# Seven half products for eight in the weight products of a four-layer graph network

## The chip, the cores and the metric
The kernel runs on one core of a Trainium2 chip. A core has a matrix engine (TensorE, PE in the profile), a vector engine (VectorE, DVE), a scalar engine (ScalarE, ACT), GpSimd (POOL) and SyncE (SP), which here only issues transfers. The metric is the device time of one launch in microseconds. Everything is float32, and N = 2708 nodes with D = 512 features are worked on.

## The reference
Four layers follow one another, and each is wrapped in a residual and a layer norm:

```python
deg = jnp.maximum((adj != 0).astype(jnp.float32).sum(-1), 1.0)
x = layernorm(x + layer0(x))   # relu((dinv*(adj + I)*dinv @ x + x) @ W0 + b0)
x = layernorm(x + layer1(x))   # (dis*adj*dis @ x) @ W1.T + b1
x = layernorm(x + layer2(x))   # twice: proj = x @ W; Wh, Ws = split(proj)
                               #   a = softmax(Wh @ Ws.T) * adj; x = leaky_relu(a @ Wh + x)
x = layernorm(x + layer3(x))   # adj @ (x @ W3) + b3, all heads side by side
```

The three dense layers (0, 1 and 3) each have one product with the sparse 2708 x 2708 adjacency and one with a 512 x 512 weight. Layer 2 has two attention layers, each with its own projection.

## The kernel before
**Chunks.** The 2708 nodes are cut into six chunks of columns (`CH`): four of 512 (called wide here), then 384 and 276 (narrow). They also form 22 blocks of 128 rows (the last one has 20). A wide chunk has four blocks. The adjacency product of a chunk goes over six groups of row blocks (`GROUPS`): `multiply(ly, k, g)` adds one group into four PSUM banks, one for each 128 of the features. It takes the rows of x split in two parts, hi and lo, and the adjacency tiles `m`, which ACT casts from bytes or from float32. PSUM is used as two halves of four banks, and the chunks take turns on them (`bank(half, name)`).

**A dense layer.** `step` does one group of one chunk. After the last group `evict` writes `ht` (the transposed result) from PSUM to SBUF. The products with the weights are not made at once: `step` calls `ends(run, phase)` for the chunk before, one phase after each group of the chunk now running. Phase 0, after the first group, is `project`: for each block of 128 rows four matmuls of 128 x 128 by 128 x 512 into a bank `mm`. It also combines the first two blocks. Phase 1, after the second group, combines the rest and calls `finish`, which normalizes and writes rows `o`. In layer 1 phase 2, after the third group, turns `o` on TensorE (`tr_x2t`) for the attention. `combine` takes a block's `mm`, scale and bias into `r`, adds the residual `xres`, and gets statistics for the norm; the root `rs_t` of the norm is an ACT instruction, and the rest is on DVE.

**Attention.** For each chunk `project_steps` makes `wst`, the product of `mixed` (a product of the two halves of W, made early) with the chunk's `xt`, in four banks of four matmuls, and then `z`, the product of `xt` with W's first half, one bank for each row block. ACT copies `wst` and `z` to SBUF. `sum_weights` then adds and subtracts quarters of `wst` on DVE, because the attention's score products (`spx`, `spy`) are made in a seven-product form already. Of the first attention layer, chunks 0 and 1 are projected at the end of layer 1 by `project`, which calls `beat` after each step, and chunks 2 to 5 at the start of the attention itself. The second attention layer's projections are spread through the first one's scores.

**Index jobs.** From layer 1 on, lists of neighbours are made in the background. `work("DVE")` and `work("PE")` let the next piece of such a job go, on DVE (`at_row`, `marks`, and smaller pieces) or on TensorE (`list`, `rank`, `rest`). `beat` calls `work` in two of three calls. A `list` product waits for the `marks` before it.

**Order.** Every engine carries out its instructions in the order in which the program issues them: `OrderedEngine` adds a dependency from each instruction to the one before it on its engine, with no semaphore. Since this helper records them all, each instruction stands at line 71 in the profile, and is told apart by its tiles. An engine that waits keeps everything behind it waiting. The order that matters is written out by hand in `step`, `ends` and `project_steps`.

```python
for i, lo, n in sorted(blocks_of(k), key=lambda b: b[2] > QW):
    ...
    ps = self.bank(k, f"mm{ly.number}_{i}")
    for c in range(DC):
        nc.tensor.matmul(ps[:n], ly.ht[k][c][:, lo : lo + n], ly.w[c], ...)
    parts.append((i, n, ps))
```

Of the kernel before, what the change touches and what calls it, by code (L numbers as in the profile page):

```python
# [8 lines left out]
FP = mybir.dt.float32  # L9
# [475 lines left out]
    return {4: (1, P), 5: (1, P)}.get(k, (2, 2 * P))  # L485


STREAMED = 4
FIRST_LANDS = 16
SOFT = NB + 2 * 2  # L490
ALONE = 18
SEVEN = [0, 1]


def lists_of(i):
# [9 lines left out]
    return 4 * columns / 2400  # L505


class Layer:


    def __init__(self, number, source, weights, bias):
        self.number, self.source, self.weights, self.bias = number, source, weights, bias
        self.hi, self.lo = [None] * NB, [None] * NB
        self.rows = [None] * NB
        self.acc, self.ht, self.done, self.part = {}, {}, {}, {}
        self.mv = {}
        self.begun = {}
        self.loaded = set()


# [10 lines left out]
class Fast:  # L531
# [18 lines left out]
    def run(self):  # L550
        kernel, nc = self.k, self.nc
        with ExitStack() as ctx:
            pool = lambda name, bufs, **kw: ctx.enter_context(
                self.tc.tile_pool(name=name, bufs=bufs, reuse_waits="tile", **kw)
            )
            self.pages, self.wides = pool("pages", PAGES), pool("wides", WIDES)
            self.small = pool("small_f", 4)
            self.banks = [pool(f"banks{h}", 4, space=PSUM) for h in range(2)]
            given = [kernel.x_in[bass.ts(i, P), :] for i in range(NB)]
            l0 = Layer(0, given, kernel.w0, kernel.b0)  # L560
            l1 = Layer(1, kernel.saved[0], kernel.w1, kernel.b1)
            l3 = Layer(3, kernel.saved[2], kernel.w3, kernel.b3)
            self.attention = attention = Attention(self)
            self.jobs, self.due, self.other, self.beats = [], None, 1, 0
            run = Run(l0, l1)
            for t in range(len(run.seq)):
                self.step(run, t)
            attention.project(attention.layers[0], 0)
            for g in range(3):
                self.ends(run, g)  # L570
                if g == 1:
                    attention.project(attention.layers[0], 1)


            run = Run(l3)
            run.seq = [(l3, k, g) for k in range(TWO) for g in range(4)]
            run.seq += [(l3, k, g) for g in (4, 5) for k in range(2)]
            run.seq += [(l3, k, g) for k in range(2, TWO) for g in (4, 5)]
            run.seq += [(l3, k, g) for k in range(TWO, len(CH)) for g in range(len(GROUPS))]
            attention.run(self.early(run))  # L580
            for j in range(*GROUPS[5]):
                l3.rows[j] = attention.made[j]
            for t in range(4 * TWO, len(run.seq)):
                self.step(run, t)

            ly, k = run.before
            parts = self.project(ly, k)
            for some in (parts[:-1], parts[-1:]):
                made = []
                for i, n, ps in some:  # L590
                    made.append((i, n, self.combine(ly, k, len(made), i, n, ps)))
                self.finish(ly, k, made)
# [141 lines left out]
    def load_weights(self, ly):  # L734
        nc = self.nc
        ly.w = []
        for c in range(DC):
            w = self.page(f"w{ly.number}_{c}")
            nc.gpsimd.dma_start(w, ly.weights[bass.ts(c, P), :])
            ly.w.append(w)  # L740
        ly.bt = self.page(f"bias{ly.number}")
        nc.gpsimd.dma_start(ly.bt, ly.bias.partition_broadcast(P))

    def load_rows(self, ly, j):
        if ly.rows[j] is None:
# [210 lines left out]
    def degree_ends(self, ly, k):  # L956
# [22 lines left out]
        for c in range(DC):  # L979
            nc.gpsimd.tensor_mul(xt[c][:, :cw], xt[c][:, :cw], dg[:, :cw])  # L980
        yield True
        for _ in self.rsqrt(self.k.dis[:, i0 : i0 + n], cnt, DEG_EPS):
            pass
        nc.vector.tensor_scalar_max(cnt, cnt, 1.0)
        nc.vector.reciprocal(self.k.rdeg[:, i0 : i0 + n], cnt)

    def evict(self, ly, k):
        nc, cw = self.nc, CH[k][1]
# [12 lines left out]
            ht.append(t)  # L1001
        del ly.acc[k]

    def project(self, ly, k):

        nc = self.nc
        parts = []

        for i, lo, n in sorted(blocks_of(k), key=lambda b: b[2] > QW):
            if n <= QW:  # L1010
                ps = self.few(
                    k,
                    f"mm{ly.number}_{i}",
                    n,
                    D,
                    lambda c: ly.ht[k][c][:, lo : lo + n],
                    lambda c: ly.w[c],
                )
                parts.append((i, n, ps))
                continue  # L1020
            ps = self.bank(k, f"mm{ly.number}_{i}")
            for c in range(DC):
                nc.tensor.matmul(
                    ps[:n],
                    ly.ht[k][c][:, lo : lo + n],
                    ly.w[c],
                    start=(c == 0),
                    stop=(c == DC - 1),
                )
            parts.append((i, n, ps))  # L1030
        return parts
# [20 lines left out]
        return x  # L1052

    def sum(self, ly, i, n, ps):
        nc, x = self.nc, ly.done.pop(("xres", i))
        if n <= QW and ly.number == 3:
            for c in range(DC):
                nc.vector.tensor_add(x[:n], x[:n], ps[c * QW : c * QW + n, :])
# [79 lines left out]
    def step(self, run, t):  # L1138
# [3 lines left out]
        self.before_products(run, t)  # L1142
        if ly.number == 0 and (k, g) == (1, 0):
            self.attention.blank()
        if ly.number == 1 and k == len(CH) - 1 and g in (2, 3, 4):
            self.attention.begin(g - 2)
        if ly.number == 0 and g == len(GROUPS) - 1:
            self.multiply(ly, k, g, ds=range(2))
            ends = self.degree_ends(ly, k)
            next(ends)  # L1150
            self.multiply(ly, k, g, ds=range(2, DC))
        else:
            self.multiply(ly, k, g)
        if g == len(GROUPS) - 1 and k in ly.begun:
            self.evict(ly, k)
        wide = CH[k][1] == BANK
        if run.before and run.phase in ((1, 3, 4, 5) if wide else (1, 5)):
            self.work("PE")
# [11 lines left out]
        if g == len(GROUPS) - 1:  # L1170
# [10 lines left out]
            while run.before and run.phase < 2:  # L1181
                self.ends(run, run.phase)
                run.phase += 1
            if k in ly.acc:
                self.evict(ly, k)
            if ly.number == 0:
                for _ in ends:
                    pass
                self.checked()
            run.before, run.phase = (ly, k), 0  # L1190
            if ly.number == 0 and k == len(CH) - 1:
                note()
                self.load_weights(run.layers[1])
            if ly.number == 1:
                self.jobs.append((k, self.index(k)))
                self.work("DVE")
# [207 lines left out]
class AttentionLayer:  # L1404
    def __init__(self, number, pairs):
        self.number, self.pairs = number, pairs
        self.w, self.mixed, self.xt, self.wst = [], [], {}, {}
        self.sums, self.streamed, self.plain = {}, {}, set()


class Attention:
# [119 lines left out]
    def project(self, ly, k):  # L1531
        for _ in self.project_steps(ly, k):
            self.f.beat()

    def project_steps(self, ly, k):

        nc, a, cw = self.nc, ly.number, CH[k][1]
        xt = ly.xt[k]
        ly.wst[k] = []
        for m in range(DC):  # L1540
# [11 lines left out]
            ly.wst[k].append(t)  # L1552
            self.advance(DC * cost(cw))
            yield True
        self.sum_weights(ly, k)
        for i, lo, n in blocks_of(k):
            z = self.page(f"z_sb{a}_{i}")
            if n <= QW:
                ps = self.f.few(
                    0, f"z{a}_{i}", n, D, lambda c: xt[c][:, lo : lo + n], lambda c: ly.w[c]  # L1560
                )
                self.f.total(z[:n], ps, n, D)
            else:
                ps = self.bank(0, f"z{a}_{i}")
            for c in range(DC if n > QW else 0):
                nc.tensor.matmul(
                    ps[:n],
                    xt[c][:, lo : lo + n],
                    ly.w[c],
                    start=(c == 0),  # L1570
                    stop=(c == DC - 1),
                )
            if n > QW and a == 0:
                nc.scalar.copy(z[:n], ps[:n])
            elif n > QW:
                nc.vector.tensor_copy(z[:n], ps[:n])
            for b in range(2):
                rows = ly.pairs[b][i * P : i * P + n, :]
                nc.sync.dma_start(
                    bass.AP(rows.tensor, rows.offset, [rows.ap[0], (PAIR, 3), (1, D)]),  # L1580
                    z[:n].unsqueeze(1).to_broadcast([n, 3, D]),
                )
            self.advance((DC if n > QW else 1) * cost(D))
            yield True


    def quarters(self, ly, k):
# [80 lines left out]
    def replace_moving(self, ch):  # L1668
# [2 lines left out]
        for c in range(2):  # L1671
            self.nc.vector.tensor_sub(ch.part["t3"][c], ch.part["b22"][c], ch.part["t3"][c])

    PRODUCTS = {
        1: ("a11", "b11"),
        2: ("a12", "b21"),
        3: ("s4", "b22"),
        4: ("a22", "t4"),
        5: ("s1", "t1"),
        6: ("s2", "t2"),  # L1680
        7: ("s3", "t3"),
    }

    def product(self, ch, t, n, out, start=False):

        b, (w, x) = t["b"], self.PRODUCTS[n]
        for c in range(2):
            self.nc.tensor.matmul(
                out,
# [609 lines left out]
```

## Time and profile before

| what | value |
|---|---|
| median of 3 runs | 2304.07 us (2301.69 to 2308.27) |
| profiled execution | 2294.53 us, span 2292.7 us |
| TensorE busy | 2247.8 us (98%) |
| DVE busy | 1477.7 us (64%) |
| ACT busy | 691.1 us (30%) |
| POOL busy | 714.4 us (31%) |
| mean granted TensorE clock | 0.995 |
| matmuls `mm` of 512 columns | 504 records, 219.5 us |
| matmuls `z` of 512 columns | 336 records, 149.3 us |
| matmuls `wst` of 512 columns | 256 records, 114.2 us |

The span is that of one profiled execution, some 0.4% shorter than the median of the timed runs. A float32 matmul leaves two records in the trace[...]. A record's duration holds its own start and drain and overlaps the next record; the distance between two starts is what it costs in a stream. A group's line gives busy time and mean duration, then the idle time of its engine just before its instructions, and what ended that idle time. `mm` is from all three dense layers, `wst` and `z` are from both attention layers.

### The profile page before, as it was taken

Reading aid. Unit: us, or ns where it says so; the run is one execution under the profiler, and the core shown is the slowest. Engines: PE = TensorE matmul, PEld = TensorE weight load, DVE = VectorE, ACT = ScalarE, POOL = GpSimd, SP = SyncE. Lnnn points to the kernel's source line nnn. Section 1 sums busy time; section 2 is a strip of 40 time slices with the busy share of each in tenths; the row PEclk is TensorE's granted clock in tenths of the full one; section 3 lists DMA queues with packets and bytes.
Section 4 is the critical chain, followed back from the end, with each engine's and each line's share of the span. In section 5 each row is a group of like instructions: output and inputs, shape, how many; then the busy total and the mean of one; then the engine's idle time right before and its main releaser. Section 6 shows DMA issues by size and latency. Waiting matters only on the chain.

```text
span 2292.7 us, 27402 instructions
## 1 busy us (share of the span) xinstructions
PE 2247.8 (98%) x9004; PEld 1383.1 (60%) x9004; DVE 1477.7 (64%) x3012; ACT 691.1 (30%) x1474; POOL 714.4 (31%) x827
## 2 busy tenths in 40 slices
PE   9999999999999999999999999999999998899997
PEld 6677777777644787443555444687443455466685
DVE  6667787786664759866577522459859778625523
ACT  7444452222111234322222200134222323331221
POOL 2333441111000000556466550000566556643000
PEclk9999999999999999999999999999999999999999
DMA  9976762222557604889699999704879799974311
GB/s 332 294 203 166 201 185 81 77 81 86 205 192 274 243 28 153 285 283 312 224 324 364 323 410 349 260 24 150 273 264 348 256 317 345 319 231 133 113 48 43
DMA packets 274761, 504.27 MB, mean 220 GB/s; under 512 B 41774, under 2 KB 133606, under 8 KB 274608
## 3 DMA queue, kind: packets, MB, share of 16 engines
q1 hardware_dynamic: 205952, 287.46, 36.1%
q0 software_dynamic: 68656, 214.96, 29.0%
q8 instruction: 73, 1.20, 0.2%
q14 instruction: 80, 0.66, 0.1%
HBM read 316.47 MB, written 185.83 MB: 219 GB/s over the span
## 4 chain that ended last, share of the span: by engine, by line
PE 77%; DVE 8%; DMA 7%; issue 3%; ACT 2%; SPq 1%; POOL 1%; another core or an unknown queue 0%; DVEq 0%; ACTq 0%; POOLq 0%
PE acc L71 28%; PE sp L71 18%; PE mm L71 8%; PE spx L71 6%; PE z L71 5%; PE wst L71 5%; PE spy L71 4%; DVE s L71 2%; DMA pairs<-s 1%; DMA at<-in_adj_t 1%; DMA g<-pairs,givers 1%; DVE sum L71 1%; SPq L71 1%; DMA xt<-t 1%; DMA x<-in_x 1%
## 5 line engine op out<-in xcount | busy, mean ns | idle before, releaser
L71 POOL DMA_INDIRECT g<-pairs,givers x510 | 532.8, 1045 | 867.8 <-issue 373.5
L71 PE MATMUL acc<-m,xh 128*128 128x512 f32 (+4 forms) x1584 | 567.3, 379 | 3.6 <-ACT m L71 2.5
L71 PE MATMUL acc<-m,xl 128*128 128x512 f32 (+4 forms) x1584 | 550.7, 365 | 6.5 <-issue 5.8
L71 PE MATMUL sp<-xs,wst_sb 128*128 128x512 f32 (+5 forms) x1472 | 523.7, 525 | 0.0
L71 PEld LDWEIGHTS sp<-xs,wst_sb 128*128 128x128 f32 (+1 forms) x1472 | 260.7, 185 | 249.7 <-issue 186.2
L71 PEld LDWEIGHTS acc<-m,xh 128*128 128x128 f32 (+1 forms) x1584 | 288.6, 188 | 67.0 <-issue 20.8
L71 PEld LDWEIGHTS acc<-m,xl 128*128 128x128 f32 (+1 forms) x1584 | 289.1, 189 | 51.3 <-issue 11.6
L71 PE MATMUL acc<-g 128*32 128x512 f32 (+1 forms) x1020 | 270.4, 606 | 6.8 <-DMA g<-pairs,givers 4.7
L71 PE MATMUL mm<-w,ht 128*128 128x512 f32 (+1 forms) x528 | 223.1, 593 | 0.0
L71 ACT COPY s<-sp 128x512 f32<-128x512 f32 (+2 forms) x172 | 87.4, 509 | 439.4 <-PE sp L71 249.2
L71 ACT CAST m<-at 128x512 fp32r<-128x512 uint8 (+5 forms) x396 | 198.9, 567 | 43.9 <-DMA at<-mask 27.1
L71 DVE TENSOR_TENSOR sum<-sum,s 128x512 f32<-128x512 f32 (+4 forms) x252 | 157.3, 624 | 58.6 <-ACT s L71 37.2
L71 DVE TENSOR_TENSOR s<-s,a 128x512 f32<-128x512 f32 (+3 forms) x264 | 166.2, 629 | 9.2
L71 PEld LDWEIGHTS acc<-g 128*32 128x32 f32 (+1 forms) x1020 | 76.0, 134 | 156.8 <-issue 117.2
L71 ACT ACTIVATE s<-s 128x512 f32<-128x512 f32 (+3 forms) x264 | 147.2, 580 | 68.5 <-DVE s L71 42.2
L71 DVE TENSOR_TENSOR s<-s,shift 128x512 f32<-128x512 f32 (+3 forms) x264 | 162.4, 619 | 6.6 <-issue 5.1
L71 PEld LDWEIGHTS mm<-w,ht 128*128 128x128 f32 (+1 forms) x528 | 95.7, 186 | 116.5 <-issue 112.2
L71 DVE TENSOR_TENSOR top<-top,s 128x512 f32<-128x512 f32 (+3 forms) x240 | 149.3, 622 | 20.0 <-ACT s L71 11.9
L71 PE MATMUL wst<-xt,mixed 128*128 128x512 f32 (+2 forms) x384 | 150.7, 545 | 1.6 <-DMA xt<-t 1.5
L71 PE MATMUL z<-w,xt 128*128 128x512 f32 (+1 forms) x352 | 151.3, 596 | 0.0
L71 POOL DMA_DIRECT2D x<-o x44 | 26.0, 597 | 324.4 <-DVE o L71 320.2
L71 PEld LDWEIGHTS wst<-xt,mixed 128*128 128x128 f32 x384 | 71.7, 190 | 74.6 <-issue 60.7
(190 smaller groups left out, 2143.4 us busy)
## 6 DMA issues: line engine op xcount, KB each, us to landing
pairs<-z_sb SPq DMA_DIRECT2D x84, 768.0 KB
pairs<-s SPq DMA_DIRECT2D x168, 256.0 KB
at<-in_adj_t SPq DMA_DIRECT2D x84, 256.0 KB
xres<-x POOLq DMA_DIRECT2D x44, 256.0 KB
x<-o POOLq DMA_DIRECT2D x43, 256.0 KB
pairs<-s SPq DMA_DIRECT2D x84, 128.0 KB
a<-mask SPq DMA_DIRECT2D x40, 256.0 KB
x<-x SPq DMA_DIRECT2D x37, 256.0 KB
```

The source lines that it names most:

```text
L71: ins = call(*args, **kw)
```

## The change
A product of two matrices, each cut into four quarters, is made with seven products of quarters where there were eight, with sums of quarters before and after. Two row blocks form a pair: their 2 x 4 matmuls of 512 columns become 7 products of 2 matmuls of 256 columns. Five of the seven need sums made ahead: s1, s2, s3, s4 of one side and t1 to t4 of the other. Two banks are used for a pair: `x` takes the products 1, 6, 7 and 4, added one after another, with a copy out after each; `y` takes 2 in its left half and 5 in its right half, which ACT copies out before 3 is added there.

- Layers 0 and 1 do this in all chunks, layer 3 in all but the last. A narrow chunk has one pair; its third block stays as it was. The new methods are `sum_weights` (t1 to t4, once a layer), `sum_rows` (s1 to s4, after each `evict`), and `project_seven`. ACT takes the copies in layers 0 and 1, with the node's scale; in layer 3 DVE adds out of PSUM straight into `xres`. `sum` then adds y, the kept product and the bias.
- In the first attention layer (`PROJECTED`) `wst` is made so in the four wide chunks and `z` in all six. `sum_sides` makes the sums of `mixed` and of W, `sum_xt` those of a chunk's `xt`; ACT copies, and DVE adds y and the kept product v.
- The order of the half products is written out for two pairs (`ORDERS[4]`), one pair and one block (`ORDERS[3]`), and one pair and the block of 20 (`ORDERS[2]`).
- The attention's loads begin one group earlier, the second part of the degree's roots in layer 0 is issued after `evict`, and one more piece of an index job is done before chunk 0 is projected.

```diff
+ORDERS = {
+    4: "1A 1B 2A 2B 5A 6A 5B 6B 7A 3A 7B 4A 3B 4B",
+    3: "1A 2A 5A D0 6A D1 D2 7A 3A D3 4A",
+    2: "1A 2A 5A 6A F 7A 3A 4A",
+}
+PROJECTED = [0]
...
+def sevens(ly, k):
+    return ly.number < 3 or k < len(CH) - 1
...
+            self.work("DVE")
+            self.other = 1
             attention.project(attention.layers[0], 0)
...
+    def sum_rows(self, ly, k):
...
+        for c in range(2):
+            nc.vector.tensor_add(a["s1"][c], a21[c], a22[c])
+        for c in range(2):
+            nc.vector.tensor_sub(a["s2"][c], a["s1"][c], a11[c])
+        for c in range(2):
+            nc.vector.tensor_sub(a21[c], a11[c], a21[c])
+        for c in range(2):
+            nc.vector.tensor_sub(a["s4"][c], a12[c], a["s2"][c])
...
+    def seventh(self, ly, k, t, n, aside):
...
+        if n == 1:
+            t["x"] = self.bank(k, f"mmx{name}")[:, :h]
+        if n == 2:
+            t["y"] = self.bank(k, f"mmy{name}")
+        out = t["x"] if n in (1, 6, 7, 4) else t["y"][:, :h] if n == 2 else t["y"][:, h:]
+        start, (w, x) = n in (1, 2, 5), PRODUCTS[n]
+        for c in range(2):
+            nc.tensor.matmul(
+                out,
+                ly.a[k][w][c][:, bass.ts(t["b"], P)],
+                ly.b[x][c],
+                start=(start and c == 0),
+                stop=(c == 1),
+                skip_group_check=not start,
+            )
+        if n in (2, 3):
+            return
+        which, to = {1: (0, 0), 6: (0, h), 7: (1, h), 4: (1, 0), 5: (1, h)}[n]
+        to = t["sums"][which][:, to : to + h]
+        if ly.number == 3:
+            nc.vector.tensor_add(to, to, out)
+            return
+        if n == 7:
+            to = t["aside"] = aside[:, t["b"], :]
+        nc.scalar.activation(to, out, AF.Copy, scale=t["scales"][which])
...
     def sum(self, ly, i, n, ps):
...
+            if which == 0:
+                nc.vector.scalar_tensor_tensor(
+                    r, t["y"], t["scales"][0], r, ALU.mult, ALU.add
+                )
+            else:
+                nc.vector.tensor_add(r[:, h:], r[:, h:], t["aside"])
+            nc.vector.tensor_add(r, r, ly.bt)
...
-        if ly.number == 1 and k == len(CH) - 1 and g in (2, 3, 4):
-            self.attention.begin(g - 2)
+        if ly.number == 1 and k == len(CH) - 1 and g in (1, 2, 3):
+            self.attention.begin(g - 1)
...
+            if ly.number == 1 and k == len(CH) - 1 and self.attention.layers[0].seven:
+                self.attention.sum_xt(self.attention.layers[0], 0)
+                sums = self.attention.sum_sides(self.attention.layers[0])
+                next(sums)
+                next(sums)
+            if k == 0 and ly.number < 3:
+                self.sum_weights(ly)
...
             if k in ly.acc:
                 self.evict(ly, k)
+                if sevens(ly, k):
+                    self.sum_rows(ly, k)
...
+    def seventh(self, t, n):
...
+        if n in to:
+            nc.scalar.copy(to[n], out)
+        if n == 3 and t["turned"]:
+            nc.vector.tensor_add(f[:, :h], f[:, :h], y[:, :h])
+            nc.vector.tensor_add(g[:, :h], g[:, :h], y[:, h:])
+        elif n == 3:
+            nc.vector.tensor_add(f, f, y)
+        if n == 4:
+            nc.vector.tensor_add(g[:, h:], g[:, h:], t["v"])
```

## The prediction, made before the changed kernel ran
> **What bounds the kernel now.** I read the page first: busy shares, the slices, the chain that ended last.
>
> ```profile
> PE 2247.8 (98%) x9004; PEld 1383.1 (60%) x9004; DVE 1477.7 (64%) x3012; ACT 691.1 (30%) x1474; POOL 714.4 (31%) x827
> PE   9999999999999999999999999999999998899997
> DVE  6667787786664759866577522459859778625523
> PE 77%; DVE 8%; DMA 7%; issue 3%; ACT 2%; SPq 1%; POOL 1%; another core or an unknown queue 0%; DVEq 0%; ACTq 0%; POOLq 0%
> ```
>
> TensorE is busy in 98% of the span, and no slice is under 8 tenths: a matmul that goes is time that goes, as long as nothing else becomes late. DVE has 36% free on average, but not in every slice. So the second look was at the groups kept apart by shape, for what a product costs on either side of the change.
>
> ```profile
> L71 PE MATMUL mm<-w,ht 128*128 128x512 f32 x504 | 219.5, 593 | 0.0
> L71 PE MATMUL z<-w,xt 128*128 128x512 f32 x336 | 149.3, 596 | 0.0
> L71 PE MATMUL wst<-xt,mixed 128*128 128x512 f32 x256 | 114.2, 596 | 1.6 <-DMA xt<-t 1.5
> L71 DVE TENSOR_TENSOR s<-s,v 128x256 f32<-128x256 f32 x40 | 16.9, 423 | 58.3 <-ACT v L71 58.3
> ```
>
> The mean of 593 ns overlaps its neighbour; the pace is the difference of starts. In the timeline 16 records of wst fill 599.07 to 605.92, 429 ns each. The score products already have the new shape:
>
> ```profile
> 788.31 1.03 PE L71 MATMUL spx<-xs,wst_sb 128*128 128x256 f32 x4
> 789.18 1.03 PE L71 MATMUL spx<-t,wst_sb 128*128 128x256 f32 x4
> 790.04 1.03 PE L71 MATMUL spx<-xs,wst_sb 128*128 128x256 f32 x4
> ```
>
> Four records take 0.865 us, 216 ns each: half of 429, with twice as many weight loads. Last, the stage where DVE has least room, in windows and in DVE's timeline:
>
> ```profile
> 578.70:667.00 88.30, 88.30 (x456) 51.00 (x454) 64.66 (x148) 16.78 (x43) 7.99 (x15) 1.00 0.53 199
> 667.00:762.00 95.00, 95.00 (x360) 47.34 (x359) 42.61 (x133) 17.05 (x36) 1.52 (x3) 1.00 0.72 262
> 599.07 3.22 DVE L71 TENSOR_TENSOR at_row<-upto,plan 128x1024 bf16<-128x1024 bf16 x3
> 603.21 3.23 DVE L71 TENSOR_TENSOR at_row<-upto,plan 128x1024 bf16<-128x1024 bf16 x3
> 610.96 0.42 DVE L71 TENSOR_TENSOR s<-wst_sb,wst_sb 128x256 f32<-128x256 f32 x1 [3.51 <-ACT wst_sb L71]
> ```
>
> From 578.7 to 667 (end of layer 1, projection of the attention's chunks 0 and 1) TensorE never stops and DVE has 23.6 us left; in the 95 us after it, 52.
>
> **What it saves.** A pair of row blocks takes 16 records x 429 = 6.86 us now and 7 products x 4 records x 216 = 6.05 us then: 0.82 us less. Pairs: layers 0 and 1 have 2 in each of four wide chunks and 1 in each of two narrow ones, 10 a layer; layer 3 leaves its last chunk alone, 9; the attention has 2 wst pairs in each of four chunks, 8, and 10 z pairs. 47 x 0.816 = 38.4 us, the most there is.
>
> A rule speaks against this. The Trainium skill, "TensorE: Matmul & The Clock Gate", section "Back-to-back issue gap", has a stream with weight loads at about 81 ns a matmul of 128 columns where the bare formula has 56: some 25 ns for the load. With 12 more records a pair that would be 0.3 us, and only 0.52 x 47 = 24 us saved. The row above decides: 216 against 429/2 = 214.5, so a load (190 ns here) still hides behind 216 ns. I take 38.4.
>
> **What it adds.** On DVE, eight 128x256 sums a wide chunk at 0.36 to 0.425 us (the row of s<-s,v has 423 ns; independent ones overlap by a tenth or more, as the four bias adds of layer 3 do, 2.46 us for 4 x 0.69), so 2.9 us between the last product of the chunk and its fifth half product; as much once a layer for the weights; 1.07 us more a pair for combining (6 operations where there were 4). Narrow chunks have 128-column sums, 2 us. In the attention a wide chunk gets 8 sums of xt and 2.3 to 2.5 us of additions for each of wst and z, about 7.7 us. On ACT, five copies of 128x256 a pair; the row s<-spx has 372 ns. An add of 256 columns out of PSUM has no row: between 0.36 (its SBUF twin) and 0.69 (512 columns out of PSUM); I take 0.42, nearest by size. The scaled copies of ACT are also without a row: not under 372, not over 585 (512 columns); 372. DMA issues on SP and POOL stay in number and queue; the stores of z only follow later additions.
>
> The cover: product 6 waits for ACT's copy of product 1, four products or 3.4 us later; 7 for that of 6, three products or 2.6 us. Four casts of m at 0.57 ahead of it, 2.3 us, still fit. Without that cover each is up to 2 us.
>
> **Boundary by boundary**, M being the start of a chunk's weight products. The first combination can begin only once the third product of a pair is in, M+8.7 rather than M+3.6, and everything queued after it on DVE moves: ACT's rs_t, which stands ahead of the m casts of the fourth adjacency group, and the rows o that TensorE turns in layer 1.
> In these lines a boundary between wide chunks could keep 1.63 us (two pairs), a narrow one 0.82; the times are M plus the durations above, in each engine's order.
> - Layer 0: between wide chunks rs_t moves from about M+18 to M+24.6, casts needed at M+26.6: 1.63 kept, twice. First boundary: already bound there by a DMA (m at 96.0), and the weights' 2.9 us come before ht: -0.3. Chunk 3 to 4, worked out: M is 227.7, ACT's rs_t comes at 245.7; with 2.9 us of sums and 2.1 of combining ahead of it on DVE, 250.9. TensorE begins the next groups 1.63 us earlier, at 239.4, has two of 5.5 us to do, and wants the fourth group's casts at 250.4; the first is there at about 251.7, 1.3 us late: +0.3. 4 to 5: -0.3. Last: +0.5. Sum 3.4 of 8.2.
> - Layer 1, first five: turn wants o at M+27.2, ready at M+26.3: 1.63 twice, 1.3 at the first. Chunk 3: wants at M+23.6, ready at about 25.5: -0.4. Sum 4.1 of 7.4.
> - 578.7 to 667, with layer 1's last boundary. New on DVE: 56 operations of 256 columns (xt sums for three chunks, 24; both weight sides, 16; additions 16) x 0.425 = 23.8; ht sums 2.3; four adds of 512 columns 2.8; combining 1.1: 30 us, on 64.7. That is 94.7 of busy time, some 88 with overlaps, where TensorE needs 81 (9 pairs less in 88.3): DVE is the bound. Placed in order: turn waits 3.2 us (-2.4 net), the first list (TensorE has it 6.9 us after wst begins, as now: 599.1 to 606.0) waits for marks whose at_row stands behind ht, its sums (2.0), the weight side's sums (2.9) and 4.2 us of an earlier list, ready 11.1 us after: 4.2; and half products wait for the bank that a DVE add must clear 1.4, 1.95 and 5.0 (behind at_row, 3.2 us each). Start of chunk 2's wst 4.5 us late. Together -6.9.
> - Chunks 2 to 5 of the attention: 5 to 14 of each 20 us busy on DVE; 7.5 of 8.2 kept.
> - Layer 3: DVE evicts itself, and the fifth product waits for ht sums and four bias adds (0.62 each): 3.3, 2.0 and 1.1 us in chunks 0 to 2, nothing later: 7.3 - 6.4 = 0.9.
>
> **The clock.** A pause of TensorE costs more than itself:
>
> ```profile
> 94.00:100.50 6.50, 4.78 (x13) 2.94 (x12) 2.52 (x6) 4.66 (x9) 0.54 (x1) 0.74 0.99 373
> 96.03 0.50 PE L71 MATMUL acc<-m,xh 128*128 128x512 f32 x1 [1.72 <-ACT m L71]
> 97.23 0.63 PE L71 MATMUL acc<-m,xl 128*128 128x512 f32 x1
> ```
>
> After 1.72 us idle, the granted clock is 0.74 over the window and starts are 430 ns apart instead of 227 until 100.4: 1.7 us lost. The same page of the skill, section "HAM oscillation", allows gaps up to about 3.4 us; by it only 4.2 and 5.0 would cost. The trace had one below that, and three others of 1.2 to 1.7 us free. By the rule 3.4 us, by "each over 1.7" some 12; but where DVE is the bound, a slow TensorE lets it catch up and the next wait shrinks. I take one, 1.7.
>
> Sum: 3.4 + 4.1 - 6.9 + 7.5 + 0.9 - 1.7 = 7.3 us. The profiled execution took 2294.53 us (2292.7 of span), so 2287.2; it lies 9.5 under the median of the runs, 2304.07, which gives 2296.8, 2297.
>
> **The rivals.**
> A, most given back, as above: 2297, own range 2288 to 2304. For it: the full DVE window. 0.59.
> B, the savings stay. DVE's free 36% takes 345 more operations; at about 0.4 us some 138 us of 815 free, waits are short because the product order leaves 2.6 to 3.4 us, and my placing is too strict in the attention and in layer 3. With half of the 22 us of waits there gone, and the clock's 1.7, it saves 7.3 + 11.1 + 1.7 = 20 us, 2284; with all of the 38.4 kept, 2266; I put it at 2277. Against it: the order on each engine is fixed, and each of those waits has a named instruction ahead of it. 0.17.
> C, slower: the handover to the attention at 578.7 to 667. If half of DVE's 23.6 us of free time there is waiting for TensorE that cannot be filled (3.51 us before s<-wst_sb is of that kind), the stage is 94.7 + 11.8 = 106.5, 18.2 longer; with three half-clock stretches, 5.1, against 15.9 gained elsewhere: 7.4 slower, 2311.5. It decides once that stage passes 88.3 + 15.9 = 104. 0.24.
> That it is not done, or not at the halved price, is excluded by spx.
>
> **How the numbers follow.** 0.3% is 6.9 us, about what a measurement of this kernel can tell from no change. A's own range straddles it: 0.33 faster, 0.26 same. With B faster 0.50; C slower 0.24. The range leaves out half of C (beyond 2313) and the better part of B (under 2281): 2281 to 2313, about 0.2.
>
> **What would show it.** Half products 216 ns apart and mm, wst, z 38 us less of TensorE. Waits of TensorE for DVE at marks, tr_x2t, wst and z between 578 and 670, 12 to 16 us, and none over 2 us in layers 0 to chunk 3; a window of that stage with DVE over 0.95. Wrong, if the stage is under 84 us (B) or over 100 (C), or if waits for ACT's copies appear.

## The result, and the profile after
The changed kernel is slower, not faster: 2309.81 us against 2303.73 us (medians of 12 runs each), a ratio of 1.0028 with a 95% interval of 1.0007 to 1.0049, that is 2 to 11 us. The prediction had said 2297: the time lies within its stated range (2281 to 2313), on the other side of the kernel before. The page of the changed kernel, in the lines that answer to those of before:

```profile
span 2320.0 us, 29165 instructions
PE 2231.2 (96%) x9568; PEld 1499.4 (65%) x9568; DVE 1606.9 (69%) x3358; ACT 752.9 (32%) x1628; POOL 710.6 (31%) x827
PE   9999999999889999999999999999999998899998
DVE  6888888897877759856677612459868778525734
```

TensorE is busy for 17 us less and DVE for 129 us more. TensorE's row now has two 8s in slices 11 and 12, which is 580 to 696 us, where the prediction had found DVE's narrowest stage. This profiled execution took 2321.77 us, 12 over its median, so its span must not be set against the 2292.7 of before; the stages can be.

The half products themselves run as predicted. In TensorE's timeline the first wide boundary of layer 0 that has no wait:

```profile
127.29 1.89 PE L71 MATMUL mmx<-w,ht 128*128 128x256 f32 x8
129.01 1.89 PE L71 MATMUL mmy<-w,ht 128*128 128x256 f32 x8
130.74 1.03 PE L71 MATMUL mmy<-t1w,s1h 128*128 128x256 f32 x4
...
138.51 1.03 PE L71 MATMUL mmx<-t4w,ht 128*128 128x256 f32 x4
139.19 0.58 PE L71 MATMUL acc<-m,xh 128*128 128x512 f32 x1
139.60 0.40 PE L71 MATMUL acc<-m,xl 128*128 128x512 f32 x1
```

The same boundary before:

```profile
123.03 13.89 PE L71 MATMUL mm<-w,ht 128*128 128x512 f32 x32
136.36 0.79 PE L71 MATMUL acc<-m,xh 128*128 128x512 f32 x1
137.00 0.40 PE L71 MATMUL acc<-m,xl 128*128 128x512 f32 x1
```

Starts are 216 ns apart, the weight loads stay hidden. The first adjacency record starts early in both traces, by less in the changed one, so I measure to the second: 12.31 us (127.29 to 139.60) where it was 13.97 (123.03 to 137.00). Two pairs save 1.66 us, as foreseen (1.63); to the first record it would look like 1.43, the 0.72 a pair of the expectations below. In the attention a pair of pairs saves 1.65 as well. The most that could be saved is 47 x 0.825 = 38.8 us.

What came back is in the list of TensorE's waits of the changed kernel (columns: what waited for what, us in total, times, longest):

```profile
PE acc L71 <- ACT m L71: 10.5, 7, 4.1
PE acc L71 <- DVE xl L71: 9.9, 4, 6.5
...
PE wst_0x L71 <- ACT wst_sb L71: 5.7, 1, 5.7
PE list L71 <- DVE marks L71: 5.1, 3, 3.3
...
PE mmx L71 <- DVE ht L71: 4.0, 2, 3.5
...
PE tr_x2t L71 <- DVE o L71: 3.8, 3, 2.5
PE spx L71 <- DVE s L71: 3.0, 1, 3.0
PE mmx L71 <- DVE xres L71: 2.8, 2, 2.5
PE z_1y L71 <- DVE wst_sb L71: 2.2, 1, 2.2
PE wst_1y L71 <- DVE z_sb L71: 2.1, 1, 2.1
```

Of these only m, xl, marks and s stood in the list of before (2.5, 0.7, 1.9 and 1.7 us); the others are new. Two of the longest are not of the change: of xl's 9.9 us, 6.5 are one wait at 1957 us, in a stage whose work stays the same, and of ACT's m, 4.1 are one wait at 2020 us, which the traces of E3 and E4 below don't have.

**What the waits cost.** TensorE's busy time (the second number after the window's length) from the start to the first dozen scores, in the kernel before, the changed one and E7, which is told below:

```profile
0.00:784.90 784.90, 777.06 (x3576) 533.61 (x3577) 554.35 (x1289) 273.33 (x586) 165.99 (x288) 1.00 0.59 189
0.00:799.70 799.70, 760.30 (x4010) 625.39 (x4011) 658.51 (x1550) 333.19 (x739) 166.44 (x288) 0.98 0.58 185
0.00:771.30 771.30, 759.29 (x3876) 591.16 (x3877) 625.15 (x1458) 310.71 (x685) 166.04 (x288) 1.00 0.60 192
```

TensorE stands still for 39.4 us where it was 7.8. These 31.6 us more are just what the 38 pairs of this stretch can save (31.4). But its busy time is only 16.8 us shorter. The other 14.6, an estimate from these figures, are products that ran longer. Some 11 of them go with the granted clock: seven windows of 7 to 13 us about the waits show 0.74 to 0.88, and the missing share times the length makes 12.5, against 1.7 for the one such window of before (an estimate too). So the waits ate the saving, and the slow stretches behind them made the loss. E7 has 25 pairs there (20.6 us), 4.2 us of new waits and 2.9 of slower products.

**Where the time went.** The same group of TensorE was looked up in each trace, and its start compared with that of before (positive: later). E1 to E8 are the experiments told below.

| landmark (us before) | after | E1 | E2 | E3 | E4 | E5 | E6 | E7 | E8 |
|---|---|---|---|---|---|---|---|---|---|
| layer 0, weight products of chunk 1 (123) | +4.3 | +0.1 | -1.3 | -2.9 | -3.0 | -1.8 | -1.2 | -0.3 | +1.5 |
| after those of chunk 3 (241) | -0.5 | -4.7 | -1.3 | -2.9 | -7.7 | -1.8 | -5.9 | -3.6 | -1.8 |
| layer 1, those of chunk 0 (354) | +8.3 | +3.6 | -1.7 | -3.4 | -0.1 | -1.6 | -4.6 | -4.0 | -2.3 |
| layer 1, those of chunk 4 (568) | +5.0 | +0.2 | -1.7 | -3.3 | -3.4 | -1.5 | -8.0 | -7.7 | -5.9 |
| products of layer 1's last chunk (628) | +8.9 | +3.5 | -4.2 | -3.4 | +0.8 | -1.7 | -10.5 | -10.2 | -6.1 |
| wst of the attention's chunk 2 (667) | +14.9 | +3.0 | +3.4 | -3.4 | +8.5 | -1.7 | -3.1 | -10.2 | -6.1 |
| first score (763) | +11.3 | +3.0 | -0.8 | -3.4 | +5.6 | -1.7 | -9.2 | -13.6 | -6.1 |
| first dozen scores (785) | +14.8 | +3.0 | +1.0 | -3.4 | +10.3 | -1.7 | -6.2 | -13.6 | -6.1 |
| change from there to 1978 | +5.2 | +12.7 | +4.0 | +6.8 | +2.7 | +1.3 | +15.3 | +6.7 | +16.9 |
| change from 1978 to the end | +8.6 | +1.7 | +2.7 | -1.8 | -1.9 | +0.1 | +1.0 | -2.9 | -1.9 |

From 785 to 1978 us (the scores, and all of the second attention layer) the change leaves the work of the engines as it is, and yet that stage took 1 to 17 us longer in all nine other traces, with no tie to what was changed that these traces show: E3 and E5, which carry the same code up to layer 3, differ there by 5.5 us. Runs of one kernel spread by some 30 us, and much of a profile's share of that seems to lie here; the profile of before was a short one. For the verdicts I use the stages on both sides of it and the medians.

The first row scatters as well. The changed kernel, E1 and E6 carry the same code up to 123 us and stand at +4.3, +0.1 and -1.2; so do E4, E7 and E8, at -3.0, -0.3 and +1.5. So 4 to 5 us there are of the single trace, and no run shows a net cost or gain of the weight sums at that boundary. The last row ends with the last instruction; the span goes on for 7.7 to 8.0 us behind it, but for 6.1 to 6.6 in the six kernels with half products in layer 3, some 1.3 us that the table doesn't show.

### The profile page after: what moved, and what is told of

It reads as the page before. It is cut to its first block, busy times and chain, and to the rows that moved or that the text cites. A ratio compares the mean times of both kernels' runs of the same rounds, so it can differ in the third digit from the quotient of the medians.

```text
span 2320.0 us, 29165 instructions
## 1 busy us (share of the span) xinstructions
PE 2231.2 (96%) x9568; PEld 1499.4 (65%) x9568; DVE 1606.9 (69%) x3358; ACT 752.9 (32%) x1628; POOL 710.6 (31%) x827
## 5 line engine op out<-in xcount | busy, mean ns | idle before, releaser
L71 PE MATMUL acc<-m,xh 128*128 128x512 f32 (+4 forms) x1584 | 567.7, 380 | 13.6 <-ACT m L71 10.5
L71 DVE TENSOR_TENSOR top<-top,s 128x512 f32<-128x512 f32 (+3 forms) x240 | 149.1, 621 | 14.8 <-ACT s L71 8.8
L71 DVE SCALAR_TENSOR_TENSOR xr<-acc,rden,xr 128x512 f32<-128x512 f32 (+1 forms) x44 | 32.8, 746 | 115.7 <-PE acc L71 109.8
L71 PE MATMUL wst<-xt,mixed 128*128 128x512 f32 (+2 forms) x256 | 94.7, 520 | 2.3 <-DMA xt<-t 1.9
L71 PE MATMUL spx<-xs,wst_sb 128*128 128x256 f32 x320 | 83.1, 383 | 3.0 <-DVE s L71 3.0
L71 ACT ACTIVATE rs_t<-rs_v 128x4 f32<-128x4 f32 (+3 forms) x31 | 6.4, 205 | 240.7 <-DVE rs_v L71 223.3
L71 DVE SCALAR_TENSOR_TENSOR odd<-at 128x512 bf16<-128x512 f32 (+2 forms) x132 | 82.4, 624 | 2.1
```

The costliest lines, as they stand in the source:

```text
L71: ins = call(*args, **kw)
```

## The experiments
**E1 to E3: one part alone.** E1 has the half products in layers 0 and 1 only, E2 in the attention only, E3 in layer 3 only; the orders that the change brings along stay in all of them.

```diff
 def sevens(ly, k):
-    return ly.number < 3 or k < len(CH) - 1
+    return ly.number < 3                           # E1, with PROJECTED = []
+    return False                                   # E2
+    return ly.number == 3 and k < len(CH) - 1      # E3, with PROJECTED = []
```

> The half products in layers 0 and 1 alone; the attention's projections and layer 3 as before. Theory A (DVE's and ACT's fixed order gives the saving back where an added DVE operation or a combination is queued ahead of what TensorE needs): layer 0 loses, by the trace of the changed kernel from the first weight products at 66 us to layer 1's first at 354 us about 8 us more than before, layer 1's chunks win back about 3; the whole comes out 3 to 6 us slower than the kernel before, and the trace shows waits of TensorE for ht (3.5), ACT's m (1.4 and 2.5) and xl (1.9 and 1.1). Theory B (the extra 27 us of the profiled execution lie in run-to-run changes of the gather and mask transfers and the change itself is nearly free): layers 0 and 1 come out 10 to 14 us faster, 20 pairs by 0.72.

> The half products in the first attention layer's projections alone; the three dense layers as before. Theory A: from the first wst to the start of chunk 2's about 7 to 10 us more than before, of which some 5.7 is TensorE's wait for ACT's copies of wst behind the norm's root rs_t of layer 1's last chunk (shorter here, because that chunk's combination is the old one, about 4); chunks 2 to 5 win back 3 to 4, the first scores lose 3 to 4 behind DVE's backlog. Whole: 5 to 9 us slower. Theory B: the 18 pairs save 13 us and the stage from 599 to 763 us is 10 us shorter.

> The half products in layer 3 alone. Theory A: waits of 2.5 and 1.8 us for DVE's xres in chunks 0 and 1 against 9 pairs by 0.72 = 6.4 us: 1 to 3 us faster, that is no difference that the runs can tell. The 4.3 us wait of TensorE for ACT's m at 2016 us in the changed kernel's trace is then not of the change and should be absent or of another size here. Theory B: 6 us faster. If the wait for m comes back at the same place with 4 us, it belongs to layer 3's part of the change.

As ratios to the kernel before: E1: 0.9986 (0.9959 to 1.0013), no difference that can be told. E2: 0.9999 (0.9973 to 1.0026), none either. E3: 0.9955 (0.9937 to 0.9972), 6 to 14 us faster. Theory A foresaw the lossy stages but not the totals: E1 is not 3 to 6 us slower, of E2's 5 to 9 only the low end is left, and E3 gained more than 1 to 3. Theory B, in which each part brings its 6 to 14 us, fails for E1 and E2: in the table E1 loses 8.2 us between 241 and 354 and wins back only 3.3 in layer 1's chunks, and E2 loses 7.6 us between 628 and 667. E3 shows that the wait for m of 4.1 us in layer 3 is not of the change (it is absent there, as in E4, and the last stage is 1.8 us shorter); the waits for xres are as the changed kernel has them, 2.5 and 1.8 us. E3's total is nearer to B's 6 us, and the orders came under suspicion (E5).

The parts don't simply add. From 568 to 628 the changed kernel loses 3.9 us, E1 loses 3.2 and E2 gains 2.5: with both, 3 us more are lost than the two would give. The wait for marks is 3.3 us in the changed kernel, 0.6 in E2, and under that in E1: the longer combination of layer 1's last chunks and the attention's additions stand in one DVE queue. By the medians the gap is wider: the three parts come to 14 us faster together, the whole is 6 slower. The stages before 785 us show some 9 of these 20, about 4 of them in the first row, which scatters.

**E4: two orders altered.** The weight sums go behind ht, and chunk 1 is projected before the last chunk of layer 1 is combined to its end.

```diff
-            if k == 0 and ly.number < 3:
-                self.sum_weights(ly)
...
                 self.evict(ly, k)
                 if sevens(ly, k):
                     self.sum_rows(ly, k)
+                if k == 0 and ly.number < 3:
+                    self.sum_weights(ly)
...
             for g in range(3):
+                if g == 1:
+                    attention.project(attention.layers[0], 1)
                 self.ends(run, g)
-                if g == 1:
-                    attention.project(attention.layers[0], 1)
```

> The changed kernel with two orders altered: the weight sums of layers 0 and 1 are issued after ht and its sums, and the attention's chunk 1 is projected before the rest of layer 1's last chunk is combined and normalized. Theory A: the wait of 3.5 us at the first weight products falls to about 1, the weight sums themselves take 3 us instead of 7 (they then don't run beside GpSimd's multiplication of xt), and the wait of 5.7 us in chunk 1's wst is gone; 5 to 8 us faster than the changed kernel, so about equal to the kernel before. Rival: DVE has the same work in that stage, the wait only moves to tr_x2t or the marks, and the whole stays within 2 us of the changed kernel.

1.0025 (1.0008 to 1.0043) to the kernel before, 2308.63 us: within 2 us of the changed kernel, so the rival holds for the whole. Stage by stage both hold. The first weight products no longer wait for ht: they start 0.7 us earlier than before, where the changed kernel starts them 3.5 later. But the second move only changed the name of the wait. In the changed kernel's ACT timeline the root of the norm holds up the copies; in E4's list of waits it is TensorE's own turn:

```profile
654.14 0.20 ACT L71 ACTIVATE rs_t<-rs_v 128x3 f32<-128x3 f32 x1 [9.00 <-DVE rs_v L71]
654.25 0.35 ACT L71 COPY wst_sb<-wst_0x 128x256 f32<-128x256 f32 x1
654.50 0.38 ACT L71 COPY wst_sb<-wst_1x 128x256 f32<-128x256 f32 x1
```

```profile
PE tr_x2t L71 <- DVE o L71: 9.9, 4, 6.1
```

wst_0x was done at 645.5, and its copy could go only after rs_t, which waited for DVE until 654. With the projection first, rs_t and o come 16 us later, and the turn waits 6.1 us. Both kernels lose 6 to 8 us between 628 and 667.

**E5: the orders alone.** No half products; the rest of the change stays.

```diff
-    return ly.number < 3 or k < len(CH) - 1
+    return False
...
-PROJECTED = [0]
+PROJECTED = []
```

> No half products at all: only the orders that the change brings with it (the second part of layer 0's degree roots after ht, the attention's loads one group earlier, one piece of an index job before chunk 0's projection). Theory A: most of the 10 us that layer 3's kernel gained is of these orders, since its traces are 3 us ahead at the second weight products (the half-clock stretch near 97 us is gone) and 4.5 us at 1123 us: 3 to 5 us faster than the kernel before. Rival: the orders are free of effect, and layer 3's half products alone give the 10 us: within 2 us of the kernel before.

1.0000 (0.9976 to 1.0025). Its trace is 1.7 us ahead at 785 us. That doesn't tell the two apart. E3's stages (3.4 and 1.8) and the 1.3 us behind its last instruction make 6.5, the low end of its interval; what it gained beyond that is not explained.

**E6: narrow chunks of layers 0 and 1 as they were.**

```diff
-    return ly.number < 3 or k < len(CH) - 1
+    return k < (len(CH) - 1 if ly.number == 3 else 4)
```

> The changed kernel, with the narrow chunks (384 and 276 columns) of layers 0 and 1 left as eight products. Theory A: a narrow chunk saves 0.6 to 0.7 us, and its next chunk has two short adjacency groups to hide the longer combination behind; the waits for ACT's m at 289 us (2.5 and half clock), for xl at 326 and 335 us (1.9 and 1.1) and for o at 591 us (2.5) and part of that for ACT's copies at 648 us go away: 8 to 12 us faster than the changed kernel, 2 to 6 faster than the kernel before. Rival: waits stay, since they come from the wide chunk before; within 3 us of the changed kernel.

0.9975 (0.9950 to 1.0001): 2296.40 us, some 12 us faster than the changed kernel, as theory A had it. Against the kernel before it is about 6 us faster, at the edge of what can be told. Four pairs fewer, 3.3 us of products more, and yet faster. Between 241 and 354 us it loses 1.3 where the changed kernel loses 8.8; between 568 and 628 it gains 2.5 where that one loses 3.9. What it leaves standing is chunk 1's projection, 628 to 667: 7.4 us lost, with the wait for ACT's copies at 3.7.

**E7 and E8: only where the saving is kept.** Read off the table: layers 0 and 1 in chunks 0 to 2, layer 3 in chunks 2 to 4, weight sums behind ht; E7 also has the attention's chunks 0, 2, 3 and 4, E8 none of the attention's.

```diff
+    return (ly.number, k) in [(0, 0), (0, 1), (0, 2), (1, 0), (1, 1), (1, 2), (3, 2), (3, 3), (3, 4)]
...
-PROJECTED = [0]
+PROJECTED = {0: (0, 2, 3, 4)}       # E8: {0: ()}
...
-        if not ly.seven:
-            yield from self.direct_z(ly, k, blocks_of(k))
+        if k not in ly.ks:
+            yield from self.direct_z(ly, k, blocks_of(k)[:-1])
+            self.sum_xt(ly, k + 1)
+            yield from self.direct_z(ly, k, blocks_of(k)[-1:])
             return
```

> Half products only where the traces show that their saving is kept: layers 0 and 1 in chunks 0 to 2, layer 3 in chunks 2 to 4, the attention's chunks 0, 2, 3 and 4; the weight sums of layers 0 and 1 after ht and its sums. Adding what each stage gave in the earlier traces: orders 3, layer 0 about 4, layer 1 about 3, attention 5, layer 3 about 4: 16 to 23 us faster than the kernel before (2283 to 2290 at a median of 2306). Rival: the stages hide one another, and the sum comes to half of that.

> As the selected version, with the attention's projections left as they were. Theory A: the attention's part of the selection is worth about 5 us, so 11 to 17 us faster than the kernel before. Rival: the attention's half products lose what they save even in the chosen chunks, and this one is as fast as the selected version or faster.

E7: 0.9916 (0.9890 to 0.9941), 2282.73 us, 14 to 25 us faster than the kernel before; the stages before 785 and after 1978 give 13.6 + 2.9 = 16.5. That is within the 16 to 23 expected. E8: 0.9978 (0.9955 to 1.0001), 2300.73 us, under the 11 to 17 us expected of it; its stages give 6.1 + 1.9 = 8. So the attention's part of the selection is worth 7.5 us by the stages before 785. The medians differ by 18; 10 of these us show between 785 and 1978, where the work is the same, and stay unexplained. E7 makes 30 of the 47 pairs so, and beats both kernels. One stage of it in a window, beside the changed kernel's, both from the end of chunk 4's weight products in layer 1 to the wst of the attention's chunk 2:

```profile
583.10:682.00 98.90, 84.98 (x564) 73.11 (x562) 86.67 (x216) 26.60 (x77) 8.04 (x15) 0.95 0.39 144
```

```profile
570.60:657.00 86.40, 85.83 (x507) 60.24 (x505) 75.49 (x184) 19.82 (x55) 8.20 (x15) 1.00 0.53 198
```

(Columns: window, its length, then busy us of PE, PEld, DVE, ACT and POOL, the granted clock, the DMAs.) The changed kernel has 11 us more of DVE work there than E7, and 0.9 us less of TensorE's; TensorE stands still for 14 us instead of 0.6.

## Why the prediction was wrong, point by point
The mechanism was named: DVE's and ACT's fixed order gives the saving back. The sum failed on size, and the sign with it. Two of its terms failed most: the clock, put at one slow stretch of 1.7 us where the granted clocks account for some 11 and all slower products for 14.6 (estimates from the windows above), and the last two boundaries of layer 0, put at -0.3 and +0.5 where they lost 3.4 and 3.2. The time fell within the stated range only because the range was wide. By its own terms, kept time positive:

- **The saving**, 38.4: right, 38.8. The half products' pace held, and the rule on weight loads didn't apply.
- **Layer 0**, +3.4 predicted, -8.3 measured to 354 us in the changed kernel, -3.6 in E1 with the same layer 0. The first boundary, put at -0.3: the weight sums took 7.1 us and not 2.9 (below), and the first products waited 3.5 us. E1 and E6 waited too (4.0 and 2.9) and had made it up by 123 us, for there TensorE didn't stop again at the next stage's m, which had held it for 1.7 us before; the changed kernel's trace paid both. Chunk 3's wait was 1.2 us, 1.3 foreseen. Chunk 4's boundary was put at -0.3: rs_v came at 291.5 us, where it had come at 284.6, and the wait for m was 2.5 us and drew a stretch of low clock; -3.4 with its own saving. The last boundary was put at +0.5 without looking at what layer 1's first groups need from DVE: xl stands behind the combination, and TensorE waited 1.9 and 1.1 us for it and 0.6 for m; -3.2. E1 and E4 lose as much at these two (3.3 and 3.4; 3.3 and 2.8), and the edit of E6 shows the cause: from 241 to 354 us it loses 1.3 without the narrow chunks' half products, and E7, without chunk 3's as well, gains 0.4. The boundaries of chunks 1 and 2 were right, 1.65 kept at each.
- **Layer 1**, +4.1 to chunk 4: +3.3. Right, the wait for o at chunk 3 included.
- **The handover**, -6.9: -9.9 (568 to 667). The waits listed for it come to 15.8 us, which against the 7.4 saved gives -8.4 and not -6.9. TensorE stood still for 13.9, less than that; about 4 us more (an estimate: 85.0 us busy for 88.3 - 7.4 expected) went into slower products. The wait for marks was 3.3 (4.2 foreseen), that for o 2.5 (3.2), z's bank 2.2 (1.95); the other two waits for banks, 1.4 and 5.0, did not come. In their place stood one for ACT, 5.7: the working followed DVE's queue and treated ACT as free, but rs_t waits in ACT's queue for DVE and takes the copies of wst with it, so product 6 found no copy of product 1. Nor was DVE the bound: it was busy for 86.7 us of 98.9, where over 0.95 was foreseen. Order, not work, held TensorE up.
- **Chunks 2 to 5**, +7.5: +3.7, with a wait of 2.1 for z_sb and a stretch of low clock behind it, and then -3.5 in the first scores, which the working had left out because their code doesn't change. The last chunk's z additions are still in DVE's queue when the first scores want t and s. E7, with chunk 5 as before, loses nothing there.
- **Layer 3**, +0.9: +1.8 (E3) and +1.9 (E4), with waits of 2.5 and 1.8 us for 3.3 and 2.0. Right there; E6 lost 1.0, and the changed kernel's own trace 8.6, with the wait of 4.1 for m. Kernels with the old layer 3 scatter from +0.1 to +2.7 in that row.
- **The clock**, -1.7: granted clocks of 0.74 to 0.86 follow six waits before 800 us in the changed kernel (65, 289, 612, 648, 710 and 786 us). The reason for taking one stretch only, that a slow TensorE lets DVE catch up, is not borne out: the some 11 us reckoned above are near the 12 of "each over 1.7" that the prediction set aside. This loss is inside the stages above.

The lines for layer 0. Behind the first boundary, the window of the changed kernel and then that of E1:

```profile
94.00:104.00 10.00, 8.04 (x29) 5.59 (x28) 7.50 (x21) 4.51 (x9) 2.83 (x5) 0.88 0.90 301
94.00:104.00 10.00, 10.00 (x45) 8.08 (x44) 9.32 (x26) 6.91 (x15) 3.40 (x6) 1.00 0.93 305
```

At chunk 4's boundary, rs_v before, then rs_v and TensorE's wait in the changed kernel:

```profile
284.56 0.17 DVE L71 TENSOR_SCALAR rs_v<-mv 128x3 f32<-128x3 f32 x1
```

```profile
291.52 0.17 DVE L71 TENSOR_SCALAR rs_v<-mv 128x3 f32<-128x3 f32 x1
292.29 0.39 PE L71 MATMUL acc<-m,xh 128*128 128x276 f32 x1 [2.54 <-ACT m L71]
```

The sum was +7.3; the stages before 785 us and the layer 3 that E3 and E4 show give -14.8 + 1.9 = -12.9, or -8.7 with E1's first boundary, and the medians -6. Rival C had the place (the handover), the sign and more than one slow stretch; its price for the handover, 18 us, was too high, and about half of the loss lay in layer 0's narrow chunks (3.4 + 3.2), which no rival had.

## What to carry to other kernels
A saving on a saturated engine is kept boundary by boundary, not in sum: list for each the first instruction behind the changed work on every in-order queue, those that merely wait (a root on ACT) as well as those that are busy, and take the change only where the next stage is long enough to hide the work that moved. Count with each wait the slower products behind it: here they cost nearly half as much again as the waits. A stage whose code is untouched can still inherit a backlog. And moving one waiting instruction out of the way moves its consumers: in E4 a wait of 5.7 us on the copies became one of 6.1 on the turn.

## What the runs showed of the hardware
**DVE stands still beside GpSimd.** The weight sums of layer 0 in DVE's timeline of the changed kernel, GpSimd's timeline in the same stretch, and DVE's in E4:

```profile
61.10 0.42 DVE L71 TENSOR_TENSOR t1w<-w 128x256 f32<-128x256 f32 x1
62.97 2.84 DVE L71 TENSOR_TENSOR t2w<-w,t1w 128x256 f32<-128x256 f32 x2
65.73 1.81 DVE L71 TENSOR_TENSOR t3w<-w,w 128x256 f32<-128x256 f32 x2
67.47 0.75 DVE L71 TENSOR_TENSOR t4w<-w,t2w 128x256 f32<-128x256 f32 x2
```

```profile
61.20 5.72 POOL L71 TENSOR_TENSOR xt<-xt,dg 128x512 f32<-128x512 f32 x4 [0.32 <-DVE cnt_sb L71]
```

```profile
69.49 0.76 DVE L71 TENSOR_TENSOR t2w<-w,t1w 128x256 f32<-128x256 f32 x2
70.16 0.76 DVE L71 TENSOR_TENSOR t3w<-w,w 128x256 f32<-128x256 f32 x2
```

Two sums take 2.84 us while GpSimd multiplies xt, and 0.75 once it has ended at 66.9. In E4, where the sums come later, all eight take 2.8 us; E1 and E6, with the order of the changed kernel, show the slow ones again (1.5 us each). GpSimd's four multiplications take 5.72 us in all beside the sums, and 5.02 in the kernel before. The Trainium skill, "SBUF — State Buffer", section "Who interferes with whom", states it: a DVE instruction with two SBUF inputs contends with a GpSimd instruction that reads SBUF, over a pair of ports that only one of them can hold at a time. The trace agrees, with 1.4 us for an operation of 0.4. In the kernel before, DVE's only work there was ht, whose first input is in PSUM (0.69 us each, as elsewhere), so the trace of before did not show it.

**The clock doesn't go by the gap's length.** After a wait of 2.54 us at 289 us the window shows 0.76, and after 2.07 us at 710 us 0.79; after 2.52 us at 591 us and 2.21 us at 666 us it shows 1.00:

```profile
289.00:296.00 7.00, 4.46 (x23) 4.21 (x23) 6.34 (x21) 4.28 (x14) 2.19 (x4) 0.76 0.45 149
591.00:600.00 9.00, 6.35 (x51) 5.94 (x50) 8.49 (x19) 5.04 (x15) 4.52 (x9) 1.00 1.00 336
666.00:676.00 10.00, 7.79 (x55) 6.53 (x54) 9.62 (x24) 2.41 (x7) 0.00 (x0) 1.00 0.04 13
710.00:718.00 8.00, 5.93 (x22) 4.45 (x21) 5.35 (x19) 0.78 (x3) 0.00 (x0) 0.79 1.05 408
```

So behind a gap of 2 to 2.5 us the clock may or may not fall; what decides between them these runs don't show.

**Scaled copies.** An ACT copy of 128x256 out of PSUM with a scale per row took 473 ns, where the plain one took 372.
